# Slot ranking by chunks of 1024 tokens, routing products one step later, and a first tile by chunks of channels

## The chip, the cores and the metric

The kernel runs on one NeuronCore of a Trainium2 chip. The metric is device time in microseconds (us): the median of several executions. Beside it there is one profiled execution, whose own time and span are given below. The engines are TensorE (PE: matmuls, and PEld for its weight loads), VectorE (DVE), ScalarE (ACT), GpSimd (POOL) and SyncE (SP, which issues most transfers). They run asynchronously and wait for each other by semaphores.

## The reference

Input is `x` of 8 x 1024 tokens with 512 channels. A modulated linear layer makes `y` of it; a shared feed-forward block and a mixture of 64 routed experts (8 for each token) are applied to `y`, and their sum is added to `x`.

```python
styles = w @ (affine_w / 16).T + affine_b            # w: condition, 8 x 256
dcoefs = rsqrt(sum((weight * styles)**2) + 1e-8)
y = clip(einsum(x * styles, weight) * dcoefs + bias, -256, 256)

shared = (silu(y @ sh_gate) * (y @ sh_up)) @ sh_down # hidden size 1024
scores = sigmoid(y @ router_w.T); sb = scores + e_bias
# 8 groups of 8 experts; a group's rank is the sum of its two best; 4 groups stay
topk_idx = top_k(where(group kept, sb, -inf), 8)
p = scores[topk_idx] / (sum + 1e-20)
routed = sum over the 8 experts e of p_e * ((silu(y @ gate_e) * (y @ up_e)) @ down_e)
out = x + shared + routed                            # expert hidden size 256
```

All is float32. Most matmuls are three products of a high and a low part in the f32r format (`hi*hi`, `hi*lo`, `lo*hi`); the split is one ACT copy (the high part) and one DVE subtraction (the low part).

## The kernel before, in words

**Stage A, conditioning** (lines 203 to 424). 16 tiles of 512 tokens, with channels on the partitions. For a tile `j`, `cond(j, m)` makes one of four blocks of 128 output channels with 48 / 4 = 12 matmuls into a PSUM bank `py` (three banks). `split_x` scales and splits the next tile's `x`, `cond_out` applies bias, demodulation `dc` and the clip, `cond_lo` makes the low part `yl`, transposes the block (`rows`) and writes it to DRAM (`y_d`, `yT_d`). `logits` and `scores` give the router's scores, one and two tiles later. In `styles` the style vector is made per 128 channels; `demod_sum` sums the squared weights between the first tile's matmuls. `route_mask(c)` finds, for 1024 tokens, which experts each token takes: ten pieces of DVE work, ended by `yield`. Four of the eight chunks (`MA = 4`) are worked off in stage A, one piece after each block from tile 4 on, and what is left of them before the last tile's `cond_lo`.

**Stage B, shared expert** (lines 740 to 1075). 128 steps `(j, c)`: a token tile `j`, and a chunk `c` of 128 hidden units. Step `i` issues on PE the 24 matmuls of `gate_up(i)`, then the 12 of `down(i - 1)`; `hidden(i)` on ACT and DVE makes the operands of `down(i)`. The first eight steps also load and split the shared weights (`load_gu`, `load_dn`); `load_y` reads the next tile of `y`. The order of PE, ACT, DVE and SP is the order in which the program is written; GpSimd's is too.

Into these steps the generator `route_slots` is woven. After each step it is advanced until the cost figures that it yields reach 4.5, or 2.5 once the writes have begun; what is over is not carried on:

```python
spent = 0.0
while i and spent < (4.5 if not writing else 2.5):
    spent += next(rgen, 9.0)
```

It first finishes the masks, then counts the tokens per expert (`rt`, line 767), lays out blocks of 512, 256 and 128 slots per expert (`ecnt`, `e6`, `odd`; lines 772 to 857), and finds the owner of each unit (`ic`, `ie`, `iexp`). Then every (token, expert) pair gets its rank among the expert's pairs. The mask lies as `[P, E, NB]`, 128 tokens by 64 experts by 64 blocks of tokens, and is ranked by eight experts at a time over all 8192 tokens: a running sum on DVE (`scan`, line 865), two products on PE into the bank `ps` (lines 888 and 889: all earlier columns, and the earlier partitions by a triangle matrix in fp32), and eight 128x512 passes on DVE (`raise_`, lines 869 to 881), which turn the rank into a slot. Each such group of eight takes a whole step (`yield 9.0`), and PE's products stand in the program where they are made, ahead of the next step's `gate_up`.

When all experts are ranked, the tokens are gone through by chunks of 1024: the eight largest entries (line 904), their scores (`q` and `w8`, eight times three passes, lines 909 to 911), and the addresses `ada` (lines 928 to 939). GpSimd writes each pair to the slot table in DRAM: 64 indirect transfers per chunk, 512 in all (`tab_d`, line 943), in bursts of eight, each of which waits for the burst before to land. After the last one, line 955 reads the table back into `tokw`, and GpSimd gathers the first rows (`xg<-y_d`, line 480).

**Stage C, routed experts** (lines 1078 to 1089). 213 units of 128, 256 or 512 slots, in an order that a planner makes from costs and due times; the first transposes and gathers of it are begun in the last three steps of stage B (`early`). Each unit loads an expert's weights, gathers rows of `y`, runs gate/up and down, and adds the weighted rows into `out` by indirect transfers.

Of the kernel before, what the change touches and what calls it, by code (L numbers as in the profile page):

```python
# [21 lines left out]
P = 128  # L22
# [41 lines left out]
def body(ctx, tc, xT, x, condT, wT, vecs, affT, rwT, ebias, wexp, shgu, shdn, cst, out):  # L64
# [19 lines left out]
    oner = pp.tile([P, P], F32R, name="oner")  # L84
    tokw = pp.tile([P, NSB, 2], I32, name="tokw")
# [14 lines left out]
    mask = rp.tile([P, E, NB], F32, name="mask")  # L100
# [49 lines left out]
    MA = 4  # L150
# [4 lines left out]
    def route_mask(c):  # L155
# [43 lines left out]
        V.tensor_scalar(mask[:, :, bs].rearrange("p e b -> p b e"), e1, -1.5 * BIG, None, ALU.is_lt)  # L199
# [3 lines left out]
    with ExitStack() as actx:  # L203
# [35 lines left out]
        dm = {}  # L239

        def styles():

            ps0 = []
            for m in range(KC):
                tag = "py" if m < KC - 1 else "psm"
                ps0.append(psa.tile([P, B], F32, name="ps0", tag=tag, bufs=3 if m < KC - 1 else 1))
                for k in range(2):
                    PE.matmul(ps0[m], lhsT=af[:, k, m * P:(m + 1) * P], rhs=cd[:, k], start=k == 0, stop=k == 1)
            for k in range(KC):
                S.copy(wh[:, k], wr[:, k])  # L250
                V.tensor_scalar(sty[:, k], ps0[k], 1.0 / 16.0, vc[:, 1, k:k + 1], ALU.mult, ALU.add)
                V.tensor_tensor(sty2[:, k], sty[:, k], sty[:, k], ALU.mult)
                sub(wl[:, k], wr[:, k], wh[:, k].bitcast(F32))
                split_x(0, k)
                GP.tensor_tensor(w2[:, k], wr[:, k], wr[:, k], ALU.mult)

        def demod_sum(k):
            if k == 0:
                dm[0] = psa.tile([B, C], F32, name="psm")
            PE.matmul(dm[0], lhsT=sty2[:, k], rhs=w2[:, k], start=k == 0, stop=k == KC - 1)  # L260
            if k == KC - 1:
                dm[1] = xa.tile([B, C], F32, name="dm", tag="lt")
                S.copy(dm[1], dm[0])

        def demodulation():
            ps1 = psa.tile([P, KC, B], F32, name="psm")
            for m in range(KC):
                PE.transpose(ps1[:, m], dm[1][:, m * P:(m + 1) * P], ident[:B, :B])
# [31 lines left out]
        def cond(j, m, each=lambda k: None):  # L300
            hs, ls = xhl[j]
            if m == 0:
                st[j] = (xa.tile([P, KC, TT], F32, name="yf"), [], [])
            yf, yh, yl = st[j]
            yh.append(yp.tile([P, TT], F32R, name="yh"))
            yl.append(yp.tile([P, TT], F32R, name="yl"))
            py = psa.tile([P, TT], F32, name="py", bufs=3)
            n = 0
            for k in range(KC):
                for w_, x_ in ((wh, hs), (wh, ls), (wl, hs)):  # L310
                    PE.matmul(py, lhsT=w_[:, k, m * P:(m + 1) * P], rhs=x_[k], start=n == 0, stop=n == 3 * KC - 1)  # L311
                    n += 1
                each(k)
            pys[j, m] = py
# [67 lines left out]
        with tc.manual_schedule(engines={ET.PE, ET.Activation, ET.DVE}):  # L382
            styles()
            for j in range(NT):
# [5 lines left out]
                for m in range(KC):  # L390
                    if j == 0 and m == 0:
                        cond(0, 0, demod_sum)
                        cond(0, 1)
                        demodulation()
                    elif j or m > 1:
                        cond(j, m)
# [3 lines left out]
                    if j or m:  # L400
                        cond_lo(j - (m == 0), (m - 1) % KC)
                    if m == 1 and j >= 2:
                        scores(j - 2)
                    elif j >= 4:
                        next(mgen, None)
                if j:
                    logits(j - 1)
                if j == 0:
                    V.tensor_copy(idr, ident)
                    V.tensor_copy(oner, ones)  # L410
                    split(rhl[:, :, 0], rhl[:, :, 1], rr)
                if j in GUA:
                    load_gu(GUA.index(j))
            for _ in mgen:
                pass
# [6 lines left out]
            scores(NT - 1)  # L422

# [316 lines left out]
    with ExitStack() as bctx:  # L740
# [16 lines left out]

        def route_slots():
# [375 lines left out]
```

## Time and profile before

| | us |
|---|---|
| median of 3 runs (3827.28 to 3830.58) | 3830.45 |
| profiled execution, its own time | 3841.71 |
| its span, first to last instruction | 3839.9 |
| TensorE busy | 3742.2 (97%) |
| VectorE, ScalarE, GpSimd busy | 2232.1, 1883.5, 2074.4 |
| stage A ends (first gate/up matmul) | 257.3 |
| first and last slot write start | 547.4, 1362.1 |
| last gate/up matmul of stage B, first transpose of stage C | 1370.7, 1380.4 |
| mean granted TensorE clock | 0.989 of full |

Busy time is time in which an engine executes something; the records of successive matmuls overlap, so a busy PE is not PE at its peak. The wait rows read "engine, what it ran, line <- what released it: total us, number, longest". A wait for several semaphores is put down to the one that came last. In the timeline, a row has start, duration, engine, line, operation, output <- inputs, count, and in brackets the idle time before and what ended it. In the table of stretches each engine has its busy time, and in brackets its instructions.

### The profile page before, as it was taken

What the parts mean: (1) busy time and instruction counts of PE and PEld (TensorE: products, weight loads), DVE (VectorE), ACT (ScalarE), POOL (GpSimd) and SP (SyncE); (2) the same over time, 40 slices, a digit from 0 to 9 for tenths busy, and PEclk for the clock granted to TensorE, in tenths of its full rate; (3) what the DMA queues carried; (4) which work ended last, traced back from release to release, by engine and by line L of the source; (5) the groups of instructions that cost most, each with busy time, mean ns of one, the idle gap of its engine ahead of it and who ended that gap; (6) DMA issues with size and microseconds to landing.
All of it is one profiled execution on the core that took longest, in us unless ns stands there. A gap on an engine that the chain in (4) does not pass through costs nothing.

```text
span 3839.9 us, 53527 instructions
## 1 busy us (share of the span) xinstructions
PE 3742.2 (97%) x19000; PEld 3123.4 (81%) x19000; DVE 2232.1 (58%) x3431; ACT 1883.5 (49%) x2884; POOL 2074.4 (54%) x1595
## 2 busy tenths in 40 slices
PE   8988999999999989999999999999999999999997
PEld 6766688888888878888888888888888888888886
DVE  6878688772222236566565655565655656656653
ACT  5552111111111136666666666665666666666664
POOL 0000026666665646666666656665655666666663
PEclk9999999999999999999999999999999999999998
DMA  7752112121211157788777766776766676766664
GB/s 225 217 155 73 33 37 64 37 64 34 59 42 51 45 181 175 157 194 182 164 173 139 167 144 132 157 140 135 158 131 129 135 135 112 138 112 115 118 118 57
DMA packets 233337, 464.19 MB, mean 121 GB/s; under 512 B 42464, under 2 KB 75232, under 8 KB 227296
## 3 DMA queue, kind: packets, MB, share of 16 engines
q0 software_dynamic: 135696, 280.15, 40.0%
q1 hardware_dynamic: 96368, 179.40, 14.9%
q8 instruction: 155, 2.54, 0.3%
q10 hardware_dynamic: 992, 1.06, 0.1%
q14 instruction: 126, 1.03, 0.1%
HBM read 532.75 MB, written 191.97 MB: 189 GB/s over the span
## 4 chain that ended last, share of the span: by engine, by line
PE 85%; DVE 5%; DMA 3%; POOL 3%; issue 2%; ACT 1%; SPq 0%; DVEq 0%; ACTq 0%; POOLq 0%; another core or an unknown queue 0%
PE pg L507 34%; PE po L527 19%; PE gu L115 14%; PE po L985 6%; PE pg L516 5%; PE pt L484 4%; POOL tab_d L943 3%; PE py L311 1%; DMA xr<-in_xT 1%; DMA tab_d<-tokw,ada 1%; DVE yl L69 1%; DVE xl L294 1%; DVE yt L351 0%; DMA yT_d<-yf 0%; PE pg L521 0%
## 5 line engine op out<-in xcount | busy, mean ns | idle before, releaser
L534 POOL DMA_INDIRECT out<-oc,tokw x532 | 943.9, 1774 | 562.3 <-ACT oc L531 258.5
L943 POOL DMA_INDIRECT tab_d<-tokw,ada x512 | 524.6, 1025 | 810.0 <-DVE ada L939 518.9
L507 PE MATMUL pg<-xh,gh 128*128 128x512 f32 (+1 forms) x2384 | 834.9, 350 | 0.0
L507 PE MATMUL pg<-xh,gl 128*128 128x512 f32 (+1 forms) x2384 | 824.0, 346 | 0.0
L507 PE MATMUL pg<-xl,gh 128*128 128x512 f32 (+1 forms) x2384 | 821.2, 344 | 0.0
L480 POOL DMA_INDIRECT xg<-y_d,tokw x532 | 596.3, 1121 | 350.6 <-PE pt L484 209.7
L69 DVE TENSOR_TENSOR gl<-wg,gh 128x1024 fp32r<-128x1024 f32 x426 | 520.3, 1223 | 121.2 <-ACT gh L495 104.4
L507 PEld LDWEIGHTS pg<-xh,gl 128*128 128x128 f32 x2384 | 450.0, 189 | 57.2
L507 PEld LDWEIGHTS pg<-xl,gh 128*128 128x128 f32 x2384 | 450.2, 189 | 55.7
L507 PEld LDWEIGHTS pg<-xh,gh 128*128 128x128 f32 x2384 | 450.2, 189 | 53.0
L495 ACT CAST gh<-wg 128x1024 fp32r<-128x1024 f32 x426 | 448.3, 1055 | 9.9 <-DMA wg<-in_wexp 5.7
L531 ACT ACTIVATE oc<-po,tokw 128x512 f32<-128x512 f32 x532 | 369.5, 694 | 153.5 <-PE po L527 131.5
L69 DVE TENSOR_TENSOR xl<-pt,xh 128x512 fp32r<-128x512 f32 x532 | 356.7, 687 | 139.6 <-ACT xh L487 99.4
L527 PE MATMUL po<-dh,hh 128*128 128x512 f32 x1064 | 426.8, 401 | 0.8 <-ACT hh L656 0.8
L527 PE MATMUL po<-dh,hl 128*128 128x512 f32 x1064 | 418.2, 393 | 0.0
L527 PE MATMUL po<-dl,hh 128*128 128x512 f32 x1064 | 415.9, 391 | 0.0
L115 PE MATMUL gu<-yl,guh 128*128 128x512 f32 x1024 | 405.5, 396 | 7.9 <-DVE yl L69 7.9
L115 PE MATMUL gu<-yh,guh 128*128 128x512 f32 x1024 | 408.0, 398 | 3.8 <-ACT yh L72 3.8
L115 PE MATMUL gu<-yh,gul 128*128 128x512 f32 x1024 | 402.2, 393 | 0.0
L654 DVE TENSOR_TENSOR hf<-hf,pg 128x512 f32<-128x512 f32 x170 | 117.0, 688 | 485.5 <-PE pg L507 481.5
L487 ACT CAST xh<-pt 128x512 fp32r<-128x512 f32 x532 | 301.3, 587 | 196.2 <-PE pt L484 85.0
L126 DVE TENSOR_TENSOR h<-h,gu 128x512 f32<-128x512 f32 x128 | 87.8, 686 | 374.9 <-PE gu L115 260.1
(232 smaller groups left out, 5820.8 us busy)
## 6 DMA issues: line engine op xcount, KB each, us to landing
wg<-in_wexp SPq DMA_DIRECT2D x213, 1024.0 KB
wd<-in_wexp SPq DMA_DIRECT2D x213, 512.0 KB
y_d<-yt SPq DMA_DIRECT2D x64, 256.0 KB
xn<-in_x SPq DMA_DIRECT2D x64, 256.0 KB
out<-xn SPq DMA_DIRECT2D x64, 256.0 KB
xr<-in_xT SPq DMA_DIRECT2D x60, 256.0 KB
yT_d<-yf SPq DMA_DIRECT2D x60, 256.0 KB
yr<-yT_d SPq DMA_DIRECT2D x60, 256.0 KB
```

Of the source, the lines that this page charges most:

```text
L69: V.tensor_tensor(o, a, b, ALU.subtract)
L115: PE.matmul(p_, lhsT=w_[:, q * KC + k], rhs=y_[k], start=n == 0, stop=n == 3 * KC - 1)
L480: queued(GP.indirect_dma_start(xg[g % RXG].bitcast(F32), None, y_d, IOA(tokw[:, u.block + s, 0:1], 0)))
L487: S.copy(xh[u.xq][:, :, s * P:(s + 1) * P], pt[g % 2].bitcast(F32))
L495: S.copy(a[u.q][:, sl], (wg, wg, wd)[c][u.kind][:, sl])
L507: PE.matmul(out, lhsT=w_[u.q][:, c:c + P], rhs=x_[u.xq][:, k, :w], start=n == 0, stop=n == 3 * KC - 1)
L516: PE.matmul(out.rearrange("p (o h) -> p o h", o=2), lhsT=x_[u.xq][:, k, :P], rhs=wv[:, k], start=n == 0 and i == 0, stop=n == 5 and i == 1)
L527: PE.matmul(po[d % 2], lhsT=h_[u.q][:, k, s * P:(s + 1) * P], rhs=w_[u.q][:, k * C:(k + 1) * C], start=n == 0, stop=n == 5)
L531: S.mul(oc[d % ROC], po[d % 2], tokw[:, u.block + s, 1:2].bitcast(F32))
L534: i_ = queued(GP.indirect_dma_start(out, IOA(tokw[:, u.block + s, 0:1], 0), oc[d % ROC], None, compute_op=ALU.add))
L943: i_ = GP.indirect_dma_start(tab_d, IOA(ad[:, b, k:k + 1], 0), tw[:, b, k], None)
L985: PE.matmul(acc[j][s], lhsT=h_[:, ts], rhs=w_[c], start=c == 0 and n == 0, stop=c == HC - 1 and n == 2)
```

## The change

Four parts, in the order of the program.

1. *First tile.* `styles` makes the first style chunk by itself and the other three at once; each chunk's `x` is split before the low part of the weights is. The first tile's four output blocks have a PSUM bank each (one of them from stage B's pool), and the loop goes over chunks of input channels outside and output blocks inside. Tile 1's `x` is loaded and split before the last chunk. The demodulation is 16 products with 8 columns each instead of four of 512 and four transposes.
2. *Masks.* Two chunks in stage A instead of four, a piece on even blocks from tile 3 on; what is left comes after the last scores. The mask lies as `[P, chunk, E, 8]`.
3. *Weaving.* Routing products on PE are put in a list (`later`) and issued after the next step's `gate_up`. The generator yields `HOP` where its next piece needs such a product, which ends the step's share. The share is a credit of 3.0 in the first eight steps, 4.8 after them and 2.5 once the writes have begun; an overdraft is carried on.
4. *Ranking.* Counts per expert and chunk (`r8`) are scanned and summed over partitions once; that gives each chunk's first rank (`base`, `first`). Then each chunk of 1024 tokens is ranked for all 64 experts, looked up, addressed and written before the next one is. The triangle product is in f32r. The owners come after the second chunk's ranking. The token numbers in `tokw` are written by one iota at the start instead of eight small ones, and `ada` becomes a ring of three tiles `ad`.

```diff
-    mask = rp.tile([P, E, NB], F32, name="mask")
+    mask = rp.tile([P, NB // 8, E, 8], F32R, name="mask")
-    MA = 4
+    MA = 2
...
             for k in range(KC):
                 S.copy(wh[:, k], wr[:, k])
-                V.tensor_scalar(sty[:, k], ps0[k], 1.0 / 16.0, vc[:, 1, k:k + 1], ALU.mult, ALU.add)
-                V.tensor_tensor(sty2[:, k], sty[:, k], sty[:, k], ALU.mult)
+                if k < 2:
+                    ks = slice(0, 1) if k == 0 else slice(1, KC)
+                    n = ks.stop - ks.start
+                    V.scalar_tensor_tensor(sty[:, ks], ps0[k], 1.0 / 16.0, vc[:, 1, ks].unsqueeze(2).to_broadcast([P, n, B]), ALU.mult, ALU.add)
+                split_x(0, k)
                 sub(wl[:, k], wr[:, k], wh[:, k].bitcast(F32))
-                split_x(0, k)
+                if k == 1:
+                    V.tensor_tensor(sty2, sty, sty, ALU.mult)
                 GP.tensor_tensor(w2[:, k], wr[:, k], wr[:, k], ALU.mult)
...
             for m in range(KC):
-                PE.transpose(ps1[:, m], dm[1][:, m * P:(m + 1) * P], ident[:B, :B])
+                for k in range(KC):
+                    PE.matmul(ps1[:, m], lhsT=w2[:, k, m * P:(m + 1) * P], rhs=sty2[:, k], start=k == 0, stop=k == KC - 1)
...
             styles()
-            for j in range(NT):
+            load_x(1)
+            for m in range(KC):
+                cond_to(0, m)
+            for k in range(KC):
+                if k == KC - 1:
+                    for q in range(KC):
+                        split_x(1, q)
+                    demodulation()
+                for m in range(KC):
+                    cond(0, m, k)
+            for m in range(KC):
+                cond_out(0, m)
+                if m:
+                    cond_lo(0, m - 1)
...
+            for j in range(1, NT):
...
-                    elif j >= 4:
+                    elif j >= 3 and m % 2 == 0:
                         next(mgen, None)
...
-            for _ in mgen:
-                pass
             cond_lo(NT - 1, KC - 1)
...
             scores(NT - 1)
+            for _ in mgen:
+                pass
...
-            for a in range(0, E, 16):
-                V.tensor_reduce(rt[:, a:a + 16], mask[:, a:a + 16], axis=AX.X, op=ALU.add)
-                yield 1.1
+            for c in range(NB // NBC):
+                V.tensor_reduce(r8[:, :, c], mask[:, c].bitcast(F32), axis=AX.X, op=ALU.add)
+                yield 0.8
+            rs = sbt.tile([P, E, NB // NBC], F32R, name="rs", tag="d2")
+            V.tensor_tensor_scan(rs.rearrange("p e c -> p (e c)"), rst, r8.rearrange("p e c -> p (e c)"), 0.0, ALU.mult, ALU.add)
             ps = psr.tile([P, 512], F32, name="ps")
+            later.append(lambda: PE.matmul(ps, lhsT=oner, rhs=rs.rearrange("p e c -> p (e c)"), start=True, stop=True))
+            yield HOP
...
-            so = scan(0)
-            yield 9.0
-            for i, a in enumerate(range(0, E, 8)):
-                if i:
-                    raise_(a - 8)
-                PE.matmul(ps, lhsT=oner, rhs=so, start=True, stop=False)
-                PE.matmul(ps, lhsT=cs[:, C_TRI:C_TRI + P], rhs=mask[:, a:a + 8].rearrange("p e b -> p (e b)"), start=False, stop=True)
-                so = scan(i + 1) if a + 8 < E else None
-                yield 9.0
-            raise_(E - 8)
-            yield 4.0
+            def count(c):
+                so = sbt.tile([P, E, 8], F32R, name="so", tag="d2")
+                V.tensor_tensor_scan(so.rearrange("p e b -> p (e b)"), rst, mask[:, c].rearrange("p e b -> p (e b)").bitcast(F32), 0.0, ALU.mult, ALU.add)
+                def over():
+                    PE.matmul(ps, lhsT=oner, rhs=so.rearrange("p e b -> p (e b)"), start=True, stop=False)
+                    PE.matmul(ps, lhsT=trir, rhs=mask[:, c].rearrange("p e b -> p (e b)"), start=False, stop=True)
+                later.append(over)
...
             for c in range(NB // 8):
-                mv = mask[:, :, bl].rearrange("p e b -> p b e")
+                mv = (yield from raise_(c)).rearrange("p e b -> p b e")
+                if c == 1:
+                    yield from owners()
+                if c < NB // 8 - 1:
+                    count(c + 1)
...
-                GP.iota(tw[:, :, :, 0], pattern=[[P, 8], [0, 8]], base=c * 8 * P, channel_multiplier=1)
...
-                ad = ada[:, c]
+                ad = sbt.tile([P, 8, K], I32, name="ad", bufs=3)
...
+                if c == 0:
+                    writing.append(True)
...
                 if i:
                     gate_up(j, c)
+                for f in later:
+                    f()
+                later.clear()
...
-                spent = 0.0
-                while i and spent < (4.5 if not writing else 2.5):
-                    spent += next(rgen, 9.0)
+                credit = min(credit, 0.0) + (0.0 if not i else 2.5 if writing else 3.0 if i < HC else 4.8)
+                while credit > 0.0:
+                    cost = next(rgen, HOP)
+                    credit = 0.0 if cost is HOP else credit - cost
```

## Prediction

> **What bounds the kernel now.** I read the page first, then a table of the engines by stretch, then TensorE's waits in the stretches where it is not full, then GpSimd's queue at the seam of the stages. Stage A (conditioning) ends at 257.3 us, stage B (shared expert, 128 steps of 36 matmuls) at 1370.7, stage C (routed experts) begins at 1380.4.
>
> ```profile
> PE 3742.2 (97%) x19000; PEld 3123.4 (81%) x19000; DVE 2232.1 (58%) x3431; ACT 1883.5 (49%) x2884; POOL 2074.4 (54%) x1595
> ```
>
> TensorE is full for 97%, so a gain can only come out of its 98 us of idle time and out of stretches at half clock. The columns below are length, busy time (instructions) of PE, PEld, DVE, ACT, POOL, clock, DMA share, GB/s.
>
> ```profile
> 0.00:32.70 32.70, 23.82 (x76) 13.96 (x77) 12.74 (x29) 11.90 (x18) 9.05 (x18) 1.00 0.78 259
> 32.70:257.30 224.60, 210.75 (x897) 165.61 (x896) 185.56 (x443) 137.94 (x229) 0.00 (x0) 0.98 0.72 206
> 257.30:273.10 15.80, 10.09 (x38) 7.76 (x37) 8.80 (x36) 2.25 (x5) 0.00 (x0) 0.78 0.33 79
> 273.10:547.40 274.30, 246.25 (x1001) 191.39 (x1000) 202.48 (x500) 53.61 (x86) 0.02 (x1) 0.94 0.17 54
> 547.40:870.00 322.60, 322.60 (x1412) 264.58 (x1411) 250.77 (x476) 58.67 (x99) 214.44 (x198) 1.00 0.18 50
> 870.00:1363.00 493.00, 493.00 (x2157) 404.70 (x2156) 116.62 (x175) 88.09 (x148) 310.06 (x315) 1.00 0.16 45
> 1363.00:1405.00 42.00, 26.97 (x115) 21.63 (x114) 16.34 (x21) 11.91 (x18) 19.19 (x20) 0.80 0.86 308
> 1405.00:3840.00 2435.00, 2408.70 (x13314) 2053.74 (x13312) 1438.78 (x1754) 1519.14 (x2285) 1521.66 (x1046) 1.00 0.70 141
> ```
>
> From 547 to 1363 PE has no idle time at all; what is lost lies before 547 and at the seam. The longest waits before 547 are on VectorE:
>
> ```profile
> PE py L311 <- DVE xl L294: 7.2, 9, 1.4
> PE gu L115 <- DVE yl L69: 5.7, 1, 5.7
> PE ps L774 <- DVE rt L767: 7.3, 1, 7.3
> PE ps L831 <- DVE e L836: 3.8, 1, 3.8
> PE ps L888 <- DVE sc L872: 3.8, 3, 2.5
> ```
>
> and the seam is set by GpSimd's 512 slot writes, which start at 547.38, when DVE has the first addresses:
>
> ```profile
> 547.38 1.14 POOL L943 DMA_INDIRECT tab_d<-tokw,ada  x1 [518.88 <-DVE ada L939]
> ...
> 1362.11 0.96 POOL L943 DMA_INDIRECT tab_d<-tokw,ada  x1 [0.30 <-issue]
> 1365.54 0.58 POOL L955 DMA_DIRECT2D tokw<-tab_d  x1 [2.47 <-DMA tab_d<-tokw,ada]
> 1374.53 1.01 POOL L480 DMA_INDIRECT xg<-y_d,tokw  x1 [8.41 <-DMA tokw<-tab_d]
> ...
> 1380.37 0.72 PE L484 MATMUL pt<-idr,xg 128*128 128x128 f32 x4 [9.25 <-DMA xg<-y_d,tokw]
> ```
>
> The reader should see one chain: first address, 815.6 us from first write to end of issue, 18.3 us from the last write over the table's landing and the first gather to the first stage C matmul. PE waits 9.25 us for it. So stage B's end is not PE's: stage C starts a fixed distance after the first address, and I must price three things: how much earlier the first address comes, how the 815.6 us change, and whether PE is there in time.
>
> **First tile (by chunks of channels).** It ends at 32.7 with 8.9 us idle (5.0 for a DMA that stays, 3.7 at the demodulation). Order within the new loop: all four output blocks take chunk 0, then chunk 1, and so on. From 8.8 us on operands are ready before PE needs them. Full speed came 6 us after steady work began (14.5 to 20.5), so from 8.8 to 16 it is about 15 matmuls at 0.43 us pitch and then 33 at 0.233: 23.7. The demodulation becomes 16 products of 8 columns, two instructions each; the nearest row is the fp32 transposes (L362, four in 0.60 us): 32 x 0.15 = 4.8, so 28.5, plus about 0.5 for the `dc` chain. Tile 1 starts near 29 instead of 32.7, and its own 3.4 us loss against 13.46 (waits of 1.42 and 0.28 and half clock after them) is half gone, as its x is split earlier. Gain 5; bounds 0 (x of tile 1, moved ahead on SP, lands late) and 8. Late next: four output blocks finish together, 4 x 1.39 us on ACT and 4 x 1.8 on DVE; the next tile needs a bank only every 2.7 us, which covers it.
>
> **Masks in stage A (4 chunks to 2).** One chunk of `route_mask` costs 12.8 us of DVE: six 128x512 passes at 0.72 pitch (4.3), four small (1.0), 14 comparisons at 0.11 (1.6), reduce and add (1.7), eight max/replace pairs at 0.455 (3.6), the mask (0.6). Three pieces a tile are 3.8 us on top of about 9.3 of own work: 13.1 of 13.46 us, and SP's queue of x loads and y writes waits behind it (SP waited 11.1 us on L194 and 8.6 on `cn`). Two pieces leave 11.9. Tiles 4 to 15 now lose 19.3 us against 13.46 each; I take 13 as gained, bounds 3 (the x loads at 0.72 DMA share hold it) and 18. The tail of the masks no longer stands before the last tile's `yl`: step 0 takes 15.8 us for some 9 us of matmuls, of which 5.7 is that wait; gain 6.
>
> Here the Trainium skill is to be weighed. TensorE: Matmul & The Clock Gate (Part 1: The HAM clock gate) has the clock halve after an idle window of about 3.4 us. The trace shows clock 0.50 from 37.6 to 41.0 after waits of only 1.42 and 0.28 us, and nine such stretches, 47.6 us, before 547. By the page's window only the stretches at the four long waits (30.6 us) would return at speed; by the trace all do. The tile losses above contain them, so I keep the trace; the page would take about 8 us off the gain.
>
> **Stage B up to the first address.** In the changed order of DVE's instructions the first address chunk (`ad`) falls in step 26, as `ada` did before. Removed from DVE before it: eight scans and carries (11.4), eight raises of eight 0.69 us rows (44.4), slot owners (3, moved later), `rt` (4.9) = 64. Added: two mask chunks (25.6), eight counts `r8` (5.5), three scans (3.8), small ones (2), one raise (5.5) = 42. DVE's 200.7 busy us between 278.7 (end of step 1's gate/up) and 547.4 become about 179, plus the 0.7 us it waits in each step for ACT's `hh` (17.8). PE needs 25 x 8.23 = 206 and 2.5 for routing products. With both so near, neither hides the other fully: the routing products now stand behind the next gate/up, so PE no longer stops in mid-chain, but the one after `rs` (step 17, after the dense mask steps) still finds DVE some 6 us late. Working through the steps: 208 for PE, 6 of such stalls, then DVE's lag in step 26 (7) and its work there (10): 231, against 268.7 measured. Gain 37; bounds 25 (lag and stalls double) and 50 (none). Sum to the first address: 5 + 13 + 6 + 37 = 61.
>
> **From the first address to the seam.** Added to DVE per chunk: a raise and a scan, 6.8 us, so chunks follow each 10.4 steps (85.6 us) instead of 5.6. GpSimd needs 102 us a chunk (815.6 / 8), so it still never starves. The ring of three `ad` tiles makes DVE wait for the writes three chunks back; chunk 7 comes 601 us after chunk 0, chunk 4's writes end after some 520: 80 us of margin, else `hidden` and then PE would queue behind it. But GpSimd is slower beside a busy DVE: 1083 ns a write while DVE was 78% busy (214.4/198), 984 ns later at 24%. The dense part now lasts 601 us at about 64%: 366 writes with 0.073 more each, 27 us, where 198 writes with 0.099 gave 20. That costs 7. A page speaks against the change here: SBUF — State Buffer (Who interferes with whom) says a DVE instruction with two SBUF inputs and a GpSimd read exclude each other for the whole instruction. Then a write meeting one waits about half of 0.69 us in 64% of cases, 0.22 each: 81 us against 53 before, a cost of 28. The trace's 0.099 is far below that, so I take 7. On PE the f32r triangle product replaces two fp32 passes (0.69 to 0.46 us a set), seven sets and the owners now fall after step 26: +4, and no cost as long as PE waits at the seam. The merged iota (nearest row L960, 1.8 us) runs on GpSimd at 27 us, 500 us before its next work; with that cover gone it costs its 1.8.
>
> **Is PE there in time?** From step 1 (273.1) to step 26 (533.7) it now loses 55 us over 25 x 8.23; of the changed kernel I expect 16 (6 of stalls, 2.5 of products, the rest lag in steps 26 to 28 and half clock). It arrives 24 + 39 - 4 = 59 earlier, at 1312. The gathers land at 1380.4 - 61 + 7 = 1326. PE waits 14 instead of 9, and the half clock after it stays. Net gain 54.
>
> Profiled execution 3841.7 (span 3839.9 and 1.8 around it) less 54 is 3788; it stands 11.3 above the median of the runs, so 3830.5 - 54 = 3776.
>
> **Rivals.** (1) The writes keep the pace of the dense part to the end: 512 x 1.629 (322.6/198) = 834, 19 more: 3795. For it: DVE is busy over 60% until step 99. (2) Stage A is held by its loads and not by the masks: its 13 goes, 3789. For it: 206 GB/s, and ACT waits for x there; against it: SP itself waits on DVE. (3) The writes are not slowed and PE's lag is absorbed, so that PE sets the seam: 14 more, 3762. (4) Slower: the shared port. Writes beside DVE would have to take 1.77 us each instead of 1.63 to eat the 61 (366 x 1.77 + 146 x 1.57 = 877 = 815.6 + 61); if a write that meets a DVE row waits out the whole of it (0.64 x 0.69 = 0.44, so 2.01 us), the writes take 965 us and the kernel 3830 - 61 + 149 = 3918. Against it: the mean beside DVE at 78% is 1083 ns, and 1775 is the longest of 512. (5) The change does not do what it says: if DVE's stages keep the first address at 547, no change.
>
> **How the numbers follow.** Likeliest case 0.53, (1) 0.13, (2) 0.13, (3) 0.13, (4) 0.06, (5) 0.02. Faster by over 0.2% (7.7 us, about what a measurement here can tell) 0.92, within 0.02, slower 0.06. The range: down to all upper bounds that PE allows (54 + 14 + 6 of stage A and start), 3756; up to stage A 3, start 0, stage B 25, writes 12 worse: 3 + 0 + 6 + 25 - 12 = 22, 3808.
>
> **What would show it.** First write near 487 us; writes lasting 820 to 830; stage A's end near 239 (257.3 less 18); no PE wait on `ps` over 6 us; a wait for `xg` at the seam of 10 to 20 us; stage C unchanged. It is wrong if the first write stays after 520, if the writes take over 850, or if PE waits inside the write stretch.

## The result, and the profile after

| | before | after |
|---|---|---|
| median, us | 3830.45 (3827.28 to 3830.58) | 3783.6 (3779.0 to 3797.2) |
| profiled execution, its own time | 3841.71 | 3781.56 |
| first gate/up matmul (stage A's end) | 257.3 | 244.4 |
| first and last slot write start | 547.4, 1362.1 | 488.8, 1306.2 |
| first transpose of stage C | 1380.4 | 1320.6 |
| TensorE busy; span less busy | 3742.2; 98 | 3719.0; 61 |

The ratio of after to before is 0.9886, with a 95% interval of 0.9859 to 0.9912: faster, by 46.9 us on the medians and by 60.1 between the two profiled executions (why the two differ stands under *Net* in the account of the prediction). The prediction was right: measured 3783.6, predicted 3776 in a range of 3756 to 3808.

The page's busy times after, and the table of stretches. Its columns are length, then busy time and instructions of PE, PEld, DVE, ACT and POOL, the granted clock, DMA share and GB/s; the stretches are cut at the same events as before (tile 1 and tile 2 begin, first gate/up, step 1, first write, DVE done with its chunks, last write, seam).

```profile
PE 3719.0 (98%) x19009; PEld 3118.8 (83%) x19009; DVE 2238.6 (59%) x3428; ACT 1884.3 (50%) x2883; POOL 2087.2 (55%) x1588
```

```profile
0.00:27.00 27.00, 21.93 (x96) 18.42 (x97) 12.51 (x24) 11.84 (x18) 7.18 (x10) 0.94 0.89 300
27.00:40.10 13.10, 13.10 (x58) 10.51 (x56) 11.84 (x24) 9.86 (x17) 0.76 (x1) 1.00 0.67 230
40.10:244.40 204.30, 194.61 (x841) 153.56 (x840) 156.85 (x345) 127.79 (x213) 0.00 (x0) 0.98 0.75 214
244.40:252.30 7.90, 7.90 (x37) 6.38 (x36) 3.17 (x6) 2.23 (x5) 0.00 (x0) 1.00 0.44 105
252.30:488.80 236.50, 232.42 (x1005) 188.20 (x1004) 181.50 (x533) 54.25 (x87) 0.01 (x1) 0.99 0.21 64
488.80:1085.00 596.20, 596.20 (x2606) 488.35 (x2605) 367.76 (x647) 108.11 (x182) 386.02 (x366) 1.00 0.18 49
1085.00:1307.00 222.00, 222.00 (x973) 182.31 (x972) 54.56 (x81) 41.19 (x69) 143.03 (x147) 1.00 0.17 49
```

Read lengths against PE's busy time. Tile 1 (second row) and step 0 (fourth) now have no idle time; stage B up to the first write lost 28.1 us (274.3 less 246.25) and now loses 4.1. The third row still has 9.7 us of idle: the tiles of stage A hardly moved. What TensorE still waits for between step 1 and the first write (engine, what it ran <- releaser: total, times, longest):

```profile
PE gu L116 <- ACT yh L72: 2.5, 1, 2.5
PE ps L775 <- DVE rs L773: 0.7, 1, 0.7
```

The 7.3, 3.8 and 3.8 us on `ps` are one wait of 0.7. The chain across the seam, GpSimd's rows and then TensorE's (start, duration, and in brackets the idle time and its releaser; the 7.63 us before the first gather are the wait for the table's read, as in the profile before, though the row names a load of `xn` that landed about then):

```profile
488.79 1.14 POOL L963 DMA_INDIRECT tab_d<-tokw,ad  x1 [455.98 <-DVE h L127]
...
1306.18 0.96 POOL L963 DMA_INDIRECT tab_d<-tokw,ad  x1 [0.30 <-issue]
1308.92 0.58 POOL L975 DMA_DIRECT2D tokw<-tab_d  x1 [1.78 <-DMA tab_d<-tokw,ad]
1317.13 1.01 POOL L481 DMA_INDIRECT xg<-y_d,tokw  x1 [7.63 <-DMA xn<-in_x]
...
1320.59 0.72 PE L485 MATMUL pt<-idr,xg 128*128 128x128 f32 x4 [11.05 <-DMA xg<-y_d,tokw]
```

The first write comes 58.6 us earlier, the writes last 2.7 longer (817.4 from first to last start, against 814.7), and the way from the last write to stage C's first transpose is 3.9 shorter (14.4 against 18.3): 59.8 at stage C's start. Of the 60.1 between the profiled executions only 0.3 lies behind it. In both profiled executions writes set the seam; TensorE waits 9 us for them before and 11 after.

### The profile page after: what moved, and what is told of

Same layout as the page of the kernel before. It is cut to its first block, busy times and chain, and to the rows that moved or that the text cites. A ratio compares the mean times of both kernels' runs of the same rounds, so it can differ in the third digit from the quotient of the medians.

```text
span 3779.8 us, 53550 instructions
## 1 busy us (share of the span) xinstructions
PE 3719.0 (98%) x19009; PEld 3118.8 (83%) x19009; DVE 2238.6 (59%) x3428; ACT 1884.3 (50%) x2883; POOL 2087.2 (55%) x1588
## 2 busy tenths in 40 slices
DMA packets 233338, 464.20 MB, mean 123 GB/s; under 512 B 42464, under 2 KB 75232, under 8 KB 227296
## 4 chain that ended last, share of the span: by engine, by line
PE 87%; DMA 3%; POOL 3%; DVE 3%; issue 2%; ACT 1%; SPq 0%; POOLq 0%; DVEq 0%; ACTq 0%
PE pg L508 35%; PE po L528 19%; PE gu L116 14%; PE po L1013 7%; PE pg L517 5%; PE pt L485 4%; POOL tab_d L963 3%; DMA xr<-in_xT 1%; DMA tab_d<-tokw,ad 1%; PE py L305 1%; DVE yl L69 0%; PE pg L522 0%; DVE yt L342 0%; ACT yf L311 0%; DVE yf L312 0%
## 5 line engine op out<-in xcount | busy, mean ns | idle before, releaser
L535 POOL DMA_INDIRECT out<-oc,tokw x532 | 955.0, 1795 | 567.0 <-ACT oc L532 247.4
L963 POOL DMA_INDIRECT tab_d<-tokw,ad x512 | 529.2, 1034 | 745.1 <-DVE h L127 460.4
L69 DVE TENSOR_TENSOR dl<-wd,dh 128x1024 fp32r<-128x1024 f32 x213 | 260.5, 1223 | 76.8 <-ACT dh L496 61.3
```

What stands on the lines that cost most here:

```text
L69: V.tensor_tensor(o, a, b, ALU.subtract)
L535: i_ = queued(GP.indirect_dma_start(out, IOA(tokw[:, u.block + s, 0:1], 0), oc[d % ROC], None, compute_op=ALU.add))
L963: i_ = GP.indirect_dma_start(tab_d, IOA(ad[:, b, k:k + 1], 0), tw[:, b, k], None)
```

## Experiments

Every kernel but the first changes the changed kernel; the first adds one part to the kernel before. Times are medians, ratios are to the kernel before in the same session.

**The first tile alone.** Only the new `styles`, `cond_to`/`cond` and the loop over chunks of channels go into the kernel before; the ranking, the mask's layout and `MA = 4` stay.

```diff
-            for j in range(NT):
+            for k in range(KC):
+                ...
+                for m in range(KC):
+                    cond(0, m, k)
+            ...
+            for j in range(1, NT):
```

> The kernel before with the new first tile alone (masks, weaving and ranking as before). Theory: the first tile is worth 9.5 us at the start of tile 2 (49.6 to 40.1), and all later work moves forward by what of it survives stage A: first gate/up matmul at about 248 instead of 257.3, first slot write at about 538, time 3821. Rival: the loads of x and not PE pace stage A, so the head start is eaten: first gate/up at 253 or later, time above 3826.

Measured: 3820.8, ratio 0.9971 (0.9959 to 0.9984). Tile 2 starts at 39.6 (49.6 before, 40.1 in the changed kernel), stage A ends at 248.8, the first write is at 537.5. So the first tile's gain is 10 us up to tile 2, and it is there whole at the first write (9.9). Tiles 2 to 15 take 209.2 us here with four chunks of masks, 204.3 in the changed kernel with two: halving the masks is worth 4.9 by this pair, and 3.4 against the 207.7 of the profile before.

This kernel's write code and what runs beside it are those of the kernel before, yet its writes last 800.7 us and not 814.7, and TensorE does not wait at the seam: its first transpose of stage C follows the matmuls of stage B without a gap (the first row has the shortest, median and longest write in ns and the first and last start):

```profile
L942 POOL DMA_INDIRECT tab_d<-tokw,ada x512: 952/958/1763, 537.5 to 1338.2; - x171
...
1361.10 0.46 PE L483 MATMUL pt<-idr,xg 128*128 128x128 f32 x4
```

So 14 us of the write chain, and the seam's wait, differ between executions of the same write code; this matters for the account below.

**Routing products at once.** Everything but the place of the routing products stays; `later` issues what it is given.

```diff
-        later = []
+        class Now(list):
+            def append(self, f):
+                f()
+
+        later = Now()
```

> The changed kernel with the routing products on PE issued where their operands are made, ahead of the next gate/up, as before (the weaving's stops stay). Theory: PE again waits for DVE at each of the 13 products, five of them before the first address; that costs 10 to 20 us before it, the first write comes at 499 to 509, later waits hide in the seam's slack, time up by 10 to 20. Rival: DVE alone paces the steps before the first address, and where PE waits makes no difference: within 4 us.

Measured: 3809.99, ratio 0.9942 (0.9925 to 0.9958), 26 us slower than the changed kernel on the medians, more than the 10 to 20 that were expected. The first write is at 504.1, 15.3 later, and the writes take 821. Stage C starts at 1347.7, 27.1 later. TensorE's waits from stage A's end to the seam in this kernel:

```profile
PE ps L862 <- DVE so L859: 17.5, 8, 5.1
PE ps L775 <- DVE rs L773: 6.3, 1, 6.3
```

The waits on `ps` are back, and a wait for `xg` is not among the rows: the waits behind the first address (13.3 of the 17.5 us) make TensorE late too, so that it reaches the seam after the gathers: they did not hide in the seam's slack. One step of distance between a product's operands and the product is worth about half of the whole change (0.0056 of 0.0114 by the ratios).

**The chain held back by six steps.** The generator waits for seven steps instead of one after `count(0)`.

```diff
             count(0)
-            yield HOP
+            for _ in range(7):
+                yield HOP
```

> The changed kernel with seven instead of one step of waiting between the counting of chunk 0 and its first addresses; nothing else differs. Theory (from its first address on, the chain of slot writes sets where stage C starts, and TensorE waits for it at the seam, 11.1 us in the changed kernel): six steps of 8.2 us put the first write 49 us later, near 538; the writes keep 817 us; the seam's wait for the gathered tokens grows from 11 to about 60 us, and the median goes from 3784 to about 3832 (3824 to 3838), with stage B's matmuls ending where they did. Rival (the gain from the first address on was TensorE's own: what it no longer waits for in stage B): the median stays within 10 us of 3784. Second rival (later writes run at the faster pace of the tail, 0.97 instead of 1.06 us each beside a VectorE that is done with its chunks): a part comes back, and the median is near 3805.

Measured: 3834.3, ratio 1.0018 (1.0011 to 1.0025), 50.7 above the changed kernel's median. The first write starts at 539.87 (51.1 later), the last at 1359.13 (53.0 later). TensorE's wait at the seam:

```profile
PE pt L485 <- DMA xg<-y_d,tokw: 63.5, 1, 63.5
```

The wait for the gathers grows from 11.1 to 63.5, by 52.4, and the span by 52.0, while stage B's last gate/up matmul starts at 1309.9 instead of 1309.2. Both rivals fall: in the changed kernel what is lost before the first write is lost at the end, us for us, and nothing comes back on the way.

**The y stores on another queue.** In `rows` the stores `y_d<-yt` are issued by GpSimd, which does little in stage A, instead of SyncE.

```diff
-                    SP.dma_start(
+                    GP.dma_start(
```

> The changed kernel with the 64 stores of y's rows (y_d<-yt) issued by GpSimd instead of SyncE. Theory: stage A's remaining tile losses (15.9 us between the start of tile 2 and the first gate/up matmul, over 13.46 us a tile) come from SP's order, where these stores wait for DVE's last transpose and the next loads of x stand behind them. Then the losses fall below 6, the first gate/up comes at about 234 instead of 244.4, and the time falls by about 10, to 3773. Rival 1: the transfers themselves are the bound (0.75 share): losses stay at 15, time 3783. Rival 2: DVE is the bound: losses stay, and GpSimd's stores make DVE no faster.

Measured: 3771.8, ratio 0.9843 (0.9826 to 0.9859). What SyncE's queue waits for in the changed kernel between 30 and 244 us comes first:

```profile
SPq L345 <- DVE yt L342: 30.7, 11, 6.5
SPq L320 <- DVE yf L312: 29.4, 15, 4.7
SPq L345 <- DVE cn L176: 6.8, 2, 5.7
```

and then the stretch from tile 2 to stage A's end in this kernel:

```profile
40.90:231.95 191.05, 190.21 (x841) 151.84 (x840) 157.74 (x346) 127.75 (x214) 36.91 (x56) 1.00 0.83 230
```

L345 is the store of `y`; it waits for VectorE, by way of `yt` or of a piece of masks that came between. The loads of later `x` tiles stand behind it in the same queue: the first of tile 4 is issued at 55.31, while VectorE is done with its buffer at 41.01; with the stores elsewhere it is issued at 42.61, its buffer being free at 42.58. The fourteen tiles then take 191.05 us instead of 204.3, 2.6 above the 188.4 of fourteen full tiles (13.46 each), and DMA moves 230 GB/s instead of 214. So stage A was neither at its bandwidth nor at VectorE's limit (158 us busy of 191): it was held by the order of one queue. The move also changes how the stores are cut into packets (204667 in this kernel, 233338 in the changed one). That this helps too is not excluded, but DMA's busy share rises with the GB/s (0.75 to 0.83), and the times of issue show the order at work.

Not all of the 12 us on the medians is stage A's. The first write is 11.0 us earlier (477.8), but the writes take 822.5, TensorE waits 16.7 us at the seam, and stage C starts only 5.3 earlier. The other 6 us lie behind TensorE's last matmul, where nothing was expected: from it to the end are 19.3 us instead of 25.1.

**No masks in stage A.**

```diff
-    MA = 2
+    MA = 0
```

> The changed kernel with no chunk of masks in stage A (MA = 0): all eight run ahead of the ranking in stage B, so that only stage A's end is to be compared; the total has no meaning for the change. In the changed kernel tile 2 starts at 40.1 and the first gate/up matmul at 244.4, which is 15.9 us over fourteen tiles of 13.46. Theory (what is left there is the wait for x loads that stand behind y stores in SyncE's queue; 13.3 of the 15.9 us went when the stores had another queue): masks still lengthen VectorE's queue, and with it the stores; without them 3 to 8 us go, and stage A ends at 236 to 241. Rival (the masks are the cause, as the prediction's sum had it): over 10 us go, and it ends before 234. Second rival (two chunks of masks cost nothing any more): it ends within 1.5 us of 244.4.

Measured, in one execution: stage A ends at 235.4, tile 2 starts at 39.7. Tiles 2 to 15 in the kernel before, with the first tile alone, and here:

```profile
49.60:257.30 207.70, 195.54 (x841) 154.01 (x840) 172.77 (x419) 127.07 (x212) 0.00 (x0) 0.98 0.72 205
39.60:248.80 209.20, 198.81 (x842) 156.03 (x841) 174.09 (x422) 128.50 (x214) 0.00 (x0) 0.97 0.74 210
39.70:235.37 195.67, 192.35 (x842) 151.74 (x840) 137.17 (x242) 128.90 (x214) 0.00 (x0) 1.00 0.79 224
```

The fourteen tiles take 8.6 us less than with two chunks, and stage A ends 9.0 earlier: between what the theory and its rival named, so that neither was sized right. The loss over 188.4 is 20.8 with four chunks, 15.9 with two, 7.3 with none, and 2.6 with two chunks and the stores on another queue. The two causes fit one chain, of which the rows above show the links: masks delay VectorE, VectorE delays the store, and the store delays the loads behind it. It can be cut at either end, and the cheap end is the queue.

**Groups of sixteen.** The last 11 us and the half clock behind them are the writes' doing: GpSimd's queue in the changed kernel waits for landings after nearly every group of eight.

```profile
POOL tab_d L963 <- DMA tab_d<-tokw,ad: 144.2, 66, 5.5
```

```diff
-    BURST = 8
+    BURST = 16
```

> The changed kernel with bursts of 16 slot writes instead of 8, so half as many waits for landing (144 us of them now). Theory (the write chain sets the start of stage C): writes last about 750 instead of 817, PE's wait of 11.1 us at the seam goes, with some of the half clock after it: 12 to 16 us less, about 3770. Rival (PE sets the seam or stage C has its own pace): no change. A second rival: more writes in flight land later, so the wait per burst doubles and the writes keep 817 us.

Measured: 4026.8, ratio 1.0522 (1.049 to 1.0555). The time is 257 us above the 3770 that were expected. In five stretches between 583 and 1375 TensorE runs at a fraction of its pace; one of them, with the stretch before it:

```profile
1069.00:1135.00 66.00, 65.36 (x286) 53.34 (x285) 40.02 (x68) 11.34 (x19) 47.60 (x46) 1.00 0.19 49
1135.00:1229.00 94.00, 45.57 (x100) 24.96 (x99) 12.63 (x24) 3.65 (x6) 63.79 (x67) 0.60 0.02 1
```

100 matmuls in 94 us, where the stretch before has 286 in 66, while GpSimd goes on writing (67 writes, one each 1.40 us). TensorE's waits from 490 to 1372 name no releaser:

```profile
PE gu L116 <- issue: 88.3, 100, 2.2
PE po L1013 <- issue: 40.2, 43, 2.2
```

The idle time is spread over single matmuls: a start in such a stretch follows the one before by 0.7, 1.4, 2.1 or 2.8 us where it is held up. VectorE falls behind with TensorE and then holds the next addresses back (162 us of GpSimd's idle time), so the writes take 881 us in spite of fewer pauses.

**Four, behind the last group but one.** Groups of four wait for the group before the last: at most eight in flight as with groups of eight, but the wait is on a write 5 us old.

```diff
-    BURST = 8
+    BURST = 4
-            burst, landed = [], []
+            burst, landed, mid = [], [], []
-                            landed[:], burst[:] = burst, []
+                            landed[:], mid[:], burst[:] = mid, burst, []
```

> The changed kernel with slot writes in groups of four that wait for the group before the last, instead of groups of eight that wait for the last one: as before at most eight are in flight, but the wait is on a write issued at least four writes (5 us) earlier, so that it is hardly ever felt and the stream has no pause. Of the stalls with sixteen in a group (140 us of TensorE idle on nothing that the profile shows) two things could be the cause. Theory A (the missing pause: 8-byte writes without a gap hold up other transfers of this core, the fetches of TensorE's instructions among them): TensorE stalls as with sixteen or worse, 100 to 300 us idle between 490 and the seam, no instruction-queue packet for stretches of 60 us and more, and the median at 3950 to 4200. Theory B (more than eight in flight is what clogs): no such stalls; the chain of writes shortens by 64 waits of 2.2 us, the seam's wait goes, and the median is at 3755 to 3775.

Measured: 3765.75, ratio 0.9835 (0.9818 to 0.9851). Theory A falls: the stream has no pause and TensorE does not stall. GpSimd's waits on landings in this kernel, and all that TensorE waits for over 0.2 us from the first write to stage C:

```profile
POOL tab_d L963 <- DMA tab_d<-tokw,ad: 6.7, 20, 0.9
PE pt L485 <- DVE xl L69: 3.6, 2, 2.3
```

144.2 us of landing waits became 6.7, the writes take 692.4 us instead of 817.4, and the wait for `xg` is gone: stage B now ends where TensorE does, and stage C starts at 1309.7 instead of 1320.6.

**Eight, behind the last group but one** (`BURST = 8` in that kernel; up to sixteen in flight), to see whether theory B, that more than eight in flight stall TensorE, holds.

> The changed kernel with slot writes in groups of eight that wait for the group before the last: at most sixteen in flight as in the kernel with groups of sixteen, but the waits come as evenly as with groups of four. Theory (what stalled TensorE with sixteen was the number of writes allowed to be in flight; with at most eight and no pause it did not stall): TensorE stalls on nothing that the profile shows for 50 us or more between 490 and the seam, a gap of over 50 us between instruction fetches, and the median is over 3850. Rival (it was groups as such, sixteen writes released at once by one wait): no stalls, and the median is that of groups of four, 3762 to 3770.

Measured: 3764.45, ratio 0.9841 (0.9826 to 0.9856), with no stall and the writes in 691.5 us. Theory B falls as well. The packets say why it had to: in every one of these kernels a write's last packet follows the write's end by 0.76 us in the median and by less than 5 at most, so that rarely more than two are in flight, whatever is allowed.

**Ten and twelve.** Ten with the stores on GpSimd, twelve in the changed kernel, and sixteen once more on another occasion.

> The changed kernel with y stores issued by GpSimd (3771.8 us with that alone) and ten slot writes to a group instead of eight. The aim is the 16.7 us that TensorE waits at the seam there, and the half clock behind it. Theory (a pause per group is enough, also at ten): 51 pauses of 2.2 us instead of 64 shorten the writes by some 25 us, the seam's wait nearly goes, and the median is 3748 to 3760. Rival (groups over eight already miss pauses, as sixteen do): TensorE shows waits on nothing over 10 us between 480 and the seam, and the median is 3775 to 3900.

> The changed kernel with groups of twelve slot writes, to bound where the stalls of sixteen begin (ten had none). If groups as such stall and grow worse with their size: 3790 to 3950 here. If sixteen alone has them, or if they were of that chip: 3760 to 3780, with the writes some 15 to 30 us shorter than the 817 of groups of eight.

> The kernel with groups of sixteen slot writes once more, on whichever chip this job gets. It was 5% slower, with TensorE idle 148 us on nothing that the profile shows, in stretches in which it ran at about half clock; since then a kernel with as few pauses (groups of four behind the last but one) and one with as many writes allowed in flight (eight behind the last but one) showed nothing of it. Theory (groups of sixteen in themselves): 4000 to 4050 again, with idle of over 100 us between 490 and the seam. Rival (the chip or the moment that run fell on): no stalls, the writes shorten by what pauses go, and the median is 3762 to 3780.

Measured: ten, 3766.9, ratio 0.9839 (0.9822 to 0.9855); no stalls, but the writes take 821.7 us, not 25 less: pauses are fewer and longer, and the wait for `xg` is still 15.4. Of the expectation's theory the missing stalls came true, both sizes failed. Twelve: 3890 (3869.5 to 3916.4), ratio 1.0139 (1.011 to 1.0168), 74 us of TensorE's idle time without a releaser. Sixteen again: 3997 to 4113 in four executions, 168 us of it. So it comes again on another chip; it begins between ten and twelve (ten was run only with the stores on GpSimd), and it was not seen where a group waits for the group before the last. Why is open: neither the missing pause nor the number allowed in flight is the cause. Late instruction fetches are unlikely: the instruction queue's 16 KB packets for TensorE come once in some 127 matmuls, but the idle time does not stand at one matmul in 127: with sixteen it is 147 waits, all but one of them 2.2 us or less.

**Both edits that helped.**

> The changed kernel with both edits that helped alone: slot writes in groups of four that wait for the group before the last (3765.8 us alone), and y stores issued by GpSimd (3771.8 alone). If the two gains lie in different stages, as their traces say (the seam's wait of 11.1 us and the half clock behind it; the loads of stage A, 12 to 14 us), they add: TensorE is then without a wait over 4 us from step 1 on, stage A ends near 231, the writes end before 1180, and the median is 3750 to 3756. Rival: the earlier start of stage B opens the seam's wait again or moves slot writes against the shared weights' loads, and less than 5 us of stage A's gain reaches the end: 3760 to 3768.

Measured: 3746.25 (3745.12 to 3748.66), ratio 0.9793 (0.978 to 0.9807). Stage A ends at 230.1, the writes run from 474.6 to 1166.2, stage C starts at 1295.3. Its page:

```profile
PE 3710.6 (99%) x19009; PEld 3115.3 (83%) x19009; DVE 2238.1 (60%) x3428; ACT 1883.3 (50%) x2883; POOL 2134.7 (57%) x1652
```

TensorE's longest single waits from stage A's end to stage C are 2.3 us. The time is 4 us below the range that was expected. By the ratios the gains add: 0.0051 and 0.0043 alone, 0.0093 together. Between the spans of this kernel and of the one with groups of four (21.4), 14.4 are there at stage C's start, all that stage A gave. The other 7.0 lie behind TensorE's last matmul, which comes 18.7 us before the end instead of 25.7. What differs in that time is GpSimd's closing of its queue:

```profile
L1163 POOLq DRAIN  x3: 50/107/5826, 3758.1 to 3764.5; - x3
L1163 POOLq DRAIN  x3: 51/107/2600, 3739.9 to 3743.1; - x3
```

The first row is with groups of four alone, the second with both edits (number, then shortest, median and longest in ns): the longest drain is 3.2 us shorter, and four instructions before it (`INC_SWDGE_SEM`) take 0.8 us each instead of 1.6. In all three kernels with the stores on GpSimd the last matmul is 18.7 to 19.3 us from the end, in the eleven others 25.1 to 26.1. Why the closing is shorter is open. Of this span 33 us are not TensorE's busy time. It beats both kernels, the changed one by 37 us on the medians.

## Why the prediction was right, step by step

- **First tile: 5 predicted, 9.5 measured** (tile 2 starts at 40.1 instead of 49.6). Tile 1 was said to start near 29; it starts at 27.0, and its own loss, of which half was to go, is gone whole (13.10 us, no idle). Alone in the kernel before, the part gives the same 10. The value lies outside the bounds of 0 to 8: the term was mis-sized.
- **Masks in stage A: 13 predicted, 3.4 measured** (the loss over 188.4 falls from 19.3 to 15.9), just inside the bounds of 3 to 18. This is the step that failed. The sum took VectorE's 13.1 us in a tile of 13.46 as the cause and expected 11.9 to free it. VectorE's busy time did fall (172.8 to 156.9 us), but the loss was made in SyncE's queue, where a store waits for VectorE and loads wait for the store. The prediction named this queue and its waits on mask pieces (11.1 and 8.6 us), but took fewer masks as the cure; with half the masks the stores still wait 30.7 us for the transposes of `y`, and the loads behind them with it. Its rival that the loads hold stage A was nearer, but by bandwidth; moving the stores shows the same loads at 230 GB/s.
- **Step 0: 6 predicted, 7.9 measured** (15.8 to 7.90; no idle is left).
- **Stage B up to the first address: 37 predicted, 37.8 measured.** The count of VectorE's rows and of the later products held, and the experiment with the products at once returns 15.3 us at the first write and the waits on `ps`. The wait after `rs` was put at 6 us and is 0.7. Sum to the first address: 61 predicted, 58.6 measured, with two errors of opposite sign in stage A (4.5 too little for the first tile, 9.6 too much for the masks). That they nearly cancel is luck.
- **The writes: 7 longer predicted, 2.7 measured** against the profiled execution before, but 16.7 against the 800.7 us of the first-tile kernel. 366 writes beside the busy VectorE take 1.055 us each (386.02/366; 0.984 + 0.073 was the estimate), the 147 after that 0.973 (143.03/147). With its pauses a write takes 1.63 us in the dense part (596.2/366) and 1.51 after it; the first-tile kernel has about the same two paces (1.64 and 1.52), but the slow one for 197 writes only. So a longer dense part does cost, more than the 7 that were put for it; the 2.7 is so small because the writes in the profiled execution before took 14 us more than the same code in the first-tile kernel. By the Trainium skill's SBUF — State Buffer (Who interferes with whom) the prediction estimated 0.22 us for a write beside the busy VectorE; here it is 0.08 (1.055 less 0.973). The slower rival needed 1.77 us a write with its pauses.
- **The seam: 14 of waiting predicted, 11.05 measured.** The gathers land 3.9 us sooner after the last write than the 18.3 taken over, and TensorE arrives at 1309.5 for 1312. That the write chain sets stage C's start in the changed kernel is shown by the kernel that is held back: 51.1 at the first write, 52.0 in the span. The rival that TensorE sets the seam is thereby excluded for this kernel; it becomes true in the one with groups of four.
- **The clock.** Of 47.6 us at half clock before the first write 13.6 are left, in three stretches: 34 went, where the trace's reading had all of them and the page's 30.6. The reading was that waits well below the idle window of 3.4 us in the Trainium skill (TensorE: Matmul & The Clock Gate, Part 1: The HAM clock gate) bring it. It holds: the longest wait left between the first matmul and the first write is 2.5 us, and the clock halves after it:

```profile
312.90:316.40 3.50, 1.12 (x5) 0.56 (x3) 0.00 (x0) 0.51 (x1) 0.00 (x0) 0.99 0.89 256
316.40:319.80 3.40, 3.24 (x7) 2.33 (x8) 2.54 (x7) 1.73 (x4) 0.00 (x0) 0.50 0.31 118
```

  Another of the three (22.8 to 26.2) has no wait before it at all: it follows the 32 matmuls of 8 columns, 3.63 us in a row, that are the new demodulation. In 11 of the 13 kernels with the new first tile the clock halves right behind them. The prediction counted these products' time (4.8 us) and nothing for the clock.

- **Net.** 54 predicted, 60.1 between the profiled executions: 6 off, which is the shorter landing (3.9) and the writes (4.3) less the first address (2.4). On the medians it is 46.9, since the profiled execution stood 11.3 above the median before and 2.0 below it after. The first-tile kernel says what the 11.3 probably are. If the usual execution of the kernel before has its writes in some 800 us too, then TensorE does not wait at the seam there: stage C starts when TensorE arrives, at 1371.1 (1380.4 less 9.25), and lasts 2455.5 us as in the first-tile kernel. After the change it starts 50.5 earlier (1320.6) and lasts 3.7 longer: a gain of 46.8. It is inferred from another kernel's trace, since there is no second one of the kernel before. By it the prediction's first reading, that the write chain and not TensorE sets stage C's start, was true of the one profiled execution and of the changed kernel, but not of the kernel before as it usually runs, and the gain of 54 was too high by that wait. That 3776 is still so near is in part luck.

## What to carry to other kernels

Find the chain that sets the end and count what is before its first link: in the changed kernel 51 us before the first slot write were 52 at the end, and putting a product one step behind its operands paid 26 us with no work removed. Where two chains reach a seam within some 10 us, one profiled execution does not say which of them usually sets it. When a queue waits on a slow engine, look at what is queued behind the waiting transfer before making the engine faster: one store moved to another queue took 13 us out of stage A, where halving the extra work on that engine had taken 3 to 5. A wait on the group before the last costs almost nothing where a wait on the last costs 2 us each time (144 us over 64 groups, down to 7).

## What the runs showed of the hardware

- Groups of twelve or sixteen indirect writes, each waiting for the group directly before it, slow TensorE to between a quarter and half of its pace for stretches of 50 to 95 us (at sixteen), at a mean clock of 0.60 to 0.85 and with waits that have no releaser (74 us in all at twelve, 145 and 168 at sixteen); groups of eight or ten, or the same stream with the wait one group further back, don't (no wait of TensorE from the first write to the seam's). The cause is open.
- A 3.4 us stretch in which TensorE was busy for 1.12 us was followed by 3.4 us at half clock; waits of 1.35 and 0.85 us standing alone were not. A share of the stretch fits these rows better than a wholly idle one; where it begins was not measured. 32 matmuls of 8 columns without a wait (3.63 us) were followed by 3.4 us at half clock too, in 11 of 13 kernels.
- An indirect write beside a VectorE that is busy for 62% took 8% longer than beside one that is busy for 25% (1.055 against 0.973 us).
- With 64 stores moved from SyncE's queue to GpSimd's, the time from TensorE's last matmul to the end of the kernel fell from 25.1 to 26.1 us (eleven kernels) to 18.7 to 19.3 (three): GpSimd's closing drain took 2.60 us instead of 5.83. The cause is open.
